# The skip count carried by the bit tile: one product per position sum instead of two, in a four-layer graph kernel

## The chip, the cores and the metric

The kernel runs on one core of a Trainium2 chip. The metric is the device time of one launch in microseconds; the median of several runs is compared. An execution under the hardware profiler gives the profile; its times are called "the profile" below. TensorE (PE) multiplies, VectorE (DVE) and ScalarE (ACT) work on tiles, SyncE (SP) issues the transfers.

## The reference

Sixteen graphs of N = 1024 nodes with D = 64 features pass through four layers, each of the form x = x + layer(relu(layernorm(x)), adj). Layers 1 to 3 are a weighted mean over neighbours, an attention with eight heads whose scores get the adjacency added, and a plain graph convolution. Layer 0 is the one that matters here. It thins the adjacency, and then takes for every node and every feature a weighted sum of the three quartiles over the node's remaining neighbours:

```python
vals = jnp.where(valid[..., None], x[:, None, :, :], big)
sv = jnp.sort(vals, axis=2)
m = valid.sum(-1)
for tau, wt in zip([0.25, 0.5, 0.75], [0.25, 0.5, 0.25]):
    pos = jnp.clip(tau * (m - 1.0), 0.0)
    lo, hi = floor(pos), ceil(pos)
    frac = pos - lo
    agg = agg + wt * (gather(sv, lo) * (1.0 - frac) + gather(sv, hi) * frac)
```

So for each node, feature and each of six positions (lo and hi of three quartiles) the kernel has to find the neighbour that has just that many smaller neighbours ahead of it.

## The kernel before, in words

Each feature of a graph is sorted once, so that every node has a rank. The 1024 ranks of a feature are cut into 64 buckets (NBK) of 16 places (BKW). For a block of 512 nodes, `group` (L704) counts by matmuls with the thinned adjacency (`valid`) how many neighbours lie in each bucket up to a given one (`cum`), and builds two halves (`c0`, `c1`) of a 16-bit word that tells which places of a bucket are occupied.

The inner work is done in 1536 steps (L776): 16 graphs x 8 groups of 8 features x 2 blocks of 512 nodes x 6 positions q. A step has three parts, and the loop of `picks` (L900) calls them for three different steps: `compare(n)`, `bits(n - 1)`, `value(n - 2)`.

- `compare` (L804) asks on VectorE which buckets lie below the wanted position (`le`), masks the two halves with it (`wa` L812, `wb` L814), and sums them over the buckets on TensorE. The PSUM tile `prep` then holds, for each node, feature and each of 16 places, the same word: its low bits are the occupied places of the right bucket, and its high bits are a count of places to skip. `val` holds the candidates' values. ScalarE copies `prep` to the float32 tile `wi`, adding 1 from a bias column (L840), and `val` to `vs` (L842).
- `bits` (L845) extracts on VectorE one bit of the word for each row: shift left by a number of the row's own (the column `to30`), and keep bit 30 alone. Read as a float, the result is 2 where the place is occupied and 0 elsewhere. TensorE then forms the position sum `pz` by two products: with `nth` (L853), which gives each row half of the sum of the bits of its block up to its own place, and a large negative number if its own place is occupied, and with `plus_k` (L854), a scaled identity applied to the high half of `wi`, which adds the skip count.
- `value` (L857) compares `pz` with one number, 97, and multiplies the value by the outcome (L861). After six positions TensorE gathers the six results (`agg`, L867).

The constants `to30`, `nth`, `plus_k` and `shifts` are made once at the start (L218 to L230 and L280 to L295). `prep`, `val` and `pz` take turns in two PSUM buffers (tag `pa`); `wi`, `bit` and some other tiles take turns in four buffers (tag `a2`).

Beside these steps run two other streams: the ranking and thinning for the next graph (`background`, L959), advanced once per step, and the layers 1 to 3 of the graph that is finished (`layers`, L1250). The last lines set the pace by hand: each step adds 0.42 to a sum that is due, and layers 1 to 3 issue pieces with prices of 0.2 to 1.0 as long as something is due (L1257 to L1261). The code gives every instruction its engine and a priority by its place; the order on each engine's queue is then settled when the program is built, with two hand-made bindings (`adjoining`, L399, keeps a run of matmuls together, and `issue_after` puts one behind another). Each engine runs its queue in that order.

Of the kernel before, what the change touches and what calls it, by code (L numbers as in the profile page):

```python
# [8 lines left out]
F32 = mybir.dt.float32  # L9
BF = mybir.dt.bfloat16  # L10
HP = mybir.dt.float16
F8 = mybir.dt.float8e4
I32 = mybir.dt.int32
I16 = mybir.dt.int16
U8 = mybir.dt.uint8
AF = mybir.ActivationFunctionType
OP = mybir.AluOpType
# [4 lines left out]
P = 128  # L22
# [6 lines left out]
KHI = 65536.0  # L29
# [4 lines left out]
FIRST = 127.0  # L34
# [4 lines left out]
def tile_preln_adj_stack(  # L39
# [30 lines left out]
    nc = tc.nc  # L70
# [8 lines left out]
    const = ctx.enter_context(tc.tile_pool(name="const", bufs=1))  # L79
# [20 lines left out]
    def pa(name, shape=(P, 512), dt=F32):  # L100
        return ps.tile(list(shape), dt, tag="pa", bufs=2, name=name)
# [22 lines left out]
    def sc(name, shape=(P, P), dt=F32):  # L124
        return scrp.tile(list(shape), dt, name=name)
# [3 lines left out]
    identf = const.tile([P, P], F32, name="identf")  # L129
# [9 lines left out]
    for b_ in range(N.bit_length() - 1):  # L139
        up = N.bit_length() - 2 - 2 * b_  # L140
        nc.vector.tensor_scalar(
            rev_b, rev_i, 1 << b_, abs(up), op0=OP.bitwise_and,
            op1=OP.logical_shift_left if up >= 0 else OP.logical_shift_right,
# [62 lines left out]
    same = scr_f[:, 1, :]  # L206
# [4 lines left out]
    fplr = bits_reversed(fpl, 4, P, "fpl")  # L211
    ppl = sc("ppl", (P, P), I32)
    nc.vector.tensor_scalar(ppl, prow_i, 15, None, op0=OP.bitwise_and)
    pplr = bits_reversed(ppl, 4, P, "ppl")
    nc.vector.tensor_scalar(pblk, prow_i, 4, None, op0=OP.logical_shift_right)
    nc.vector.tensor_tensor(same, pblk, fblk, OP.is_equal)

    to30 = const.tile([P, 1], I32, name="to30")  # L218
    nc.vector.tensor_scalar(to30, pplr[:, 0:1], 15.0, None, op0=OP.add)


    tri = scr_f[:, 2, :]
    nc.vector.tensor_tensor(tri, pplr, fplr, OP.is_le)
    nc.vector.tensor_tensor(tri, tri, same, OP.mult)
    nc.vector.tensor_scalar(tri, tri, 0.5, None, op0=OP.mult)
    nth = const.tile([P, P], BF, name="nth")
    nc.vector.scalar_tensor_tensor(nth, identf, -32.0, tri, op0=OP.mult, op1=OP.add)

    plus_k = const.tile([P, P], BF, name="plus_k")
    nc.vector.tensor_scalar(plus_k, identf, 1.0 / KHI, None, op0=OP.mult)  # L230


    sel_t = const.tile([P, 2, 32], F32, name="sel_t")
# [43 lines left out]
    nc.vector.tensor_scalar(bkt, prow_i[:, 0:1], 1, None, op0=OP.logical_shift_right)  # L277
    nc.vector.tensor_scalar(off[:, 0:1], bkt, 8.0, -SHIFT, op0=OP.mult, op1=OP.add)
    nc.vector.tensor_scalar(off[:, 1:2], bkt, 0.0, None, op0=OP.is_equal)
    shifts = const.tile([P, 7], F32, name="shifts")  # L280
    nc.vector.tensor_scalar(
        shifts[:, 0:1], off[:, 0:1], -1.0, None, op0=OP.mult
    )
# [7 lines left out]
    )  # L291
    nc.vector.tensor_scalar(shifts[:, 3:4], shifts[:, 2:3], FINE, None, op0=OP.mult)
    nc.vector.memset(shifts[:, 4:5], -0.5)
    nc.vector.memset(shifts[:, 5:6], 1.0)
    nc.vector.memset(shifts[:, 6:7], 2.0 * (160.0 - FIRST) + 2.0)  # L295

    def at_row(dst, terms):

# [97 lines left out]
    def act(out_, in_, func=AF.Copy, **kw):  # L396
        nc.scalar.activation(out_, in_, func, **kw)  # L397

    def adjoining(made):  # L399

        first = next(made)
        with tc.issue_after(first.ins), tc.high_priority():
            for _ in made:
                pass
# [213 lines left out]
    def positions(valid):  # L618

        m1 = sb.tile([P, N], I16, tag="m1", bufs=1, name="m1")
        for t in range(NH):
            pm = pa("pm")
            adjoining(
                nc.tensor.matmul(pm, ones, valid[t][:, j, :], start=j == 0, stop=j == C - 1)
                for j in range(C)
            )  # L630
            nc.vector.tensor_scalar(m1[:, t * 512 : (t + 1) * 512], pm, -1.0, None, op0=OP.add)
            if t < NH - 1:
                yield None
        n6 = a2("n6", (P, N), I16)
        nc.vector.tensor_scalar(n6, m1, q_tau, q_add, op0=OP.mult, op1=OP.add)
        nc.vector.tensor_scalar(n6, n6, 3, None, op0=OP.logical_shift_right)
        kq = sb.tile([P, N], HP, tag="kq", bufs=2, name="kq")
        nc.scalar.copy(kq, n6)
        yield kq
        krow = []  # L640
        for q in range(NQ):

            krow.append(sb.tile([P, N], I16, tag="krow", bufs=NQ, name="krow"))
            for t in range(NH):
                hs = slice(t * 512, (t + 1) * 512)
                pk = pb("pkr")
                nc.tensor.matmul(pk, sel_q[:, q, :], kq[:, hs], start=True, stop=True)
                act(krow[q][:, hs], pk, AF.Identity, scale=-2.0 / KHI, bias=shifts[:, 6:7])
            if q < NQ - 1:
                yield None  # L650
        yield krow
        nr = a2("nr", (P, N), I16)
        nc.vector.tensor_scalar(nr, m1, r_tau, None, op0=OP.mult)
        nc.vector.tensor_scalar(nr, nr, 3, None, op0=OP.bitwise_and)
        coef = sb.tile([P, N], BF, tag="coef", bufs=1, name="coef")
        nc.vector.tensor_scalar(coef, nr, w_frac, w_one, op0=OP.mult, op1=OP.add)
        yield coef
# [112 lines left out]
    def picks():  # L770
# [33 lines left out]
        def compare(n):  # L804
            b, g, t, q = steps[n]
            el = els[b]
            hs = slice(t * 512, (t + 1) * 512)
            cum, c1, c0 = tables[b, g, t]
            le = a4("le", (P, 4, 512), HP)
            nc.vector.tensor_tensor(le, cum, bc(el.krow[q][:, None, hs], [P, 4, 512]), OP.is_lt)  # L810
            wa = a4("wa", (P, 4, 512), HP)
            nc.vector.tensor_tensor(wa, le, c0, OP.mult)  # L812
            wb = a4("wb", (P, 4, 512), HP)
            last = nc.vector.tensor_tensor(wb, le, c1, OP.mult)  # L814
            while owing:
                owing.pop()(last)
            prep, val = pa("prep"), pa("val")

            rounds = [
                (prep, [sel_w[:, 1, :]] * 4, [wb[:, pp, :] for pp in range(4)]),  # L820
                (prep, [sel_w[:, 0, :]] * 4, [wa[:, pp, :] for pp in range(4)]),
            ] + [
                (val, [el.tab[:, i, 4 * g + pp, :] for pp in range(4)], [le[:, pp, :] for pp in range(4)])
                for i in range(2)
            ]
            nc.tensor.matmul(
                prep, sel_q[:, q, :], el.kq[:, hs], start=True, stop=False, skip_group_check=True
            )

            def made():  # L830
                for i, (dst, w, r) in enumerate(rounds):
                    for pp in range(4):
                        yield nc.tensor.matmul(  # L833
                            dst[32 * pp : 32 * pp + 32, :], w[pp], r[pp], start=i == 2, stop=i in (1, 3),
                            tile_position=(0, 32 * pp), skip_group_check=True,
                        )

            adjoining(made())
            wi = a2("wi")
            act(wi, prep, AF.Identity, bias=shifts[:, 5:6])  # L840
            vs = sb.tile([P, 512], F32, tag="v", bufs=7, name="vs")
            act(vs, val, AF.Copy, scale=1.0 / UP)  # L842
            state[n] = [wi, vs]

        def bits(n):  # L845
            wi, vs = state[n]
            bit = a2("bit", dt=I32)
            nc.vector.tensor_scalar(  # L848
                bit, wi.bitcast(I32), to30, 0x40000000, op0=OP.logical_shift_left, op1=OP.bitwise_and
            )  # L850
            pz = pa("pz")
            up = lambda x: x.bitcast(BF).rearrange("p (n two) -> p n two", two=2)[:, :, 1]
            nc.tensor.matmul(pz, nth, up(bit), start=True, stop=False)  # L853
            nc.tensor.matmul(pz, plus_k, up(wi), start=False, stop=True)  # L854
            state[n] = [pz, vs]

        def value(n):  # L857
            b, g, t, q = steps[n]
            el = els[b]
            pz, vs = state.pop(n)  # L860
            nc.vector.scalar_tensor_tensor(vs, pz, 97.0, vs, op0=OP.is_equal, op1=OP.mult)  # L861
            vs_of[q] = vs
            if q < NQ - 1:
                return
            agg = pb("agg")
            adjoining(
                nc.tensor.matmul(  # L867
                    agg[32 * (q_ % 4) : 32 * (q_ % 4) + 32, :], sel_t[:, q_ // 4, :], vs_of[q_],
                    start=q_ < 4, stop=q_ > 1, tile_position=(0, 32 * (q_ % 4)),
                    skip_group_check=True,  # L870
                )
                for q_ in range(NQ)
            )
            def weigh(behind):
                hs = slice(t * 512, (t + 1) * 512)
                w = a2("w")
                with tc.issue_after(behind.ins) if behind else ExitStack():
                    nc.vector.tensor_tensor(w, agg, el.coef[:, hs], OP.mult)
                acc = pb("acc", (8, 512))
                nc.tensor.matmul(acc, sel_c, w, start=True, stop=True)  # L880
                nc.scalar.copy(w[:8, :], acc)
                nc.sync.dma_start(el.z[t * D + 8 * g : t * D + 8 * g + 8, t, :], w[:8, :])

            owing.append(weigh)
# [15 lines left out]
        for n in range(last + 2):  # L900
            b, g, t, q = steps[min(n, last - 1)]
# [397 lines left out]
```

## Time and profile before

| what | us |
|---|---|
| median of three runs | 12745.85 |
| lowest, highest | 12739.58, 12749.53 |
| the profiled execution | 12739.76 |
| its span, first to last instruction | 12738.0 |
| setup and first graph's preparation | 0 to 360 |
| the 1536 steps, with layers 1 to 3 beside them | 360 to 12320 |
| layers of the last graph | 12320 to 12738 |

A group's row gives the line, the engine and operation, the tile written and the tiles read, shape and type of both, the count, the busy time in us, the mean duration of one in ns, and then the time for which the engine stood idle just before these instructions and what ended it. `L397` is the line of a helper through which all activations go, so they are told apart by their tiles. A matmul's duration is a modelled latency: a following matmul starts before it is over.

### The profile page before, as it was taken

How to read it: one execution, taken by the hardware profiler on the slowest of the kernel's cores; microseconds unless marked ns; L12 is line 12 of the kernel's file. 1: busy time of each engine (PE TensorE's matmuls, PEld its weight loads, DVE VectorE, ACT ScalarE, POOL GpSimd, SP SyncE). 2: the span in 40 equal slices, each digit the busy share in tenths (PEclk: the TensorE clock that was granted, in tenths of full speed). 3: DMA queues.
4: the chain of work that ended last, by engine and by line, in shares of the span. 5: the costliest groups of instructions: out<-in, count | busy, mean ns of one | idle time of the engine just before them, and what ended most of it. 6: DMA issues, size and time to landing. Idle time of an engine off the chain costs nothing.

```text
span 12738.0 us, 220547 instructions
## 1 busy us (share of the span) xinstructions
PE 11508.7 (90%) x86209; PEld 5414.4 (43%) x86209; DVE 11510.5 (90%) x19675; ACT 9625.0 (76%) x17026; POOL 1.4 (0%) x10
## 2 busy tenths in 40 slices
PE   0789999999899998999999999999999999999988
PEld 0224444444444444444444444444444444444445
DVE  8999989899898989989899998999989899887863
ACT  0557877777777787778877788787777778788866
POOL 0000000000000000000000000000000000000000
PEclk9999999999999999999999999999999999999999
DMA  3012121221212112121221212112121121202021
GB/s 105 29 41 71 52 89 56 72 72 55 83 54 94 54 55 85 51 92 57 68 72 59 88 55 81 60 62 83 55 84 56 62 84 57 94 30 70 28 71 60
DMA packets 503192, 841.31 MB, mean 66 GB/s; under 512 B 238720, under 2 KB 273664, under 8 KB 502144
## 3 DMA queue, kind: packets, MB, share of 16 engines
q1 hardware_dynamic: 502144, 827.20, 20.2%
q8 instruction: 675, 11.06, 0.4%
q14 instruction: 373, 3.06, 0.1%
HBM read 616.27 MB, written 206.57 MB: 65 GB/s over the span
## 4 chain that ended last, share of the span: by engine, by line
DVE 29%; PE 28%; ACT 10%; issue 5%; DMA 1%; SPq 0%; DVEq 0%; ACTq 0%
DVE wa L812 5%; PE px L726 4%; DVE wb L814 4%; DVE le L810 4%; DVE s L1191 4%; PE ao L1203 3%; PE pcols L450 2%; ACT s L397 2%; DVE vs L861 2%; PE sp L1182 2%; PE prep L833 2%; PE val L833 2%; DVE bit L848 2%; PE agg L867 1%; PE two L1069 1%
## 5 line engine op out<-in xcount | busy, mean ns | idle before, releaser
L812 DVE TENSOR_TENSOR wa<-le,c 128x2048 f16<-128x2048 f16 x1536 | 1878.1, 1223 | 250.2 <-PE prep L833 190.0
L726 PE MATMUL px<-valid,cw 128*128 128x512 fp8e4 x8192 | 1977.2, 381 | 0.0
L810 DVE TENSOR_TENSOR le<-cum,krow 128x2048 f16<-128x2048 int16 x1536 | 1875.1, 1221 | 11.0 <-PE val L833 8.9
L814 DVE TENSOR_TENSOR wb<-le,c 128x2048 f16<-128x2048 f16 x1536 | 1876.6, 1222 | 1.5 <-PE prep L833 1.5
L397 ACT ACTIVATE c<-px,shifts 128x512 f16<-128x512 f32 x2048 | 1414.2, 695 | 308.6 <-PE px L747 162.8
L397 ACT ACTIVATE wi<-prep,shifts 128x512 f32<-128x512 f32 x1536 | 1066.7, 694 | 357.7 <-PE prep L833 271.4
L397 ACT ACTIVATE s<-s,nm 128x1024 f32<-128x1024 f32 x1024 | 1168.2, 1143 | 211.5 <-DVE nm L1191 202.1
L726 PEld LDWEIGHTS <-cw 128*128 128x128 f16 x8192 | 799.8, 98 | 1094.2 <-issue 202.7
L1182 PE MATMUL sp<-kT,qT 64*128 64x512 f32 x4096 | 1164.7, 642 | 69.2 <-DVE nm L1191 67.7
L450 PE MATMUL pcols<-identf,s 128*128 128x128 f32 x8192 | 1130.6, 280 | 105.4 <-ACT eT L453 57.6
L397 ACT ACTIVATE high<-px,shifts 128x512 f16<-128x512 f32 x1024 | 713.0, 696 | 653.0 <-PE px L726 650.4
L861 DVE SCALAR_TENSOR_TENSOR vs<-pz,vs 128x512 f32<-128x512 f32 x1536 | 1057.8, 689 | 161.1 <-PE pz L854 140.1
L450 PEld LDWEIGHTS pcols<-identf,s 128*128 128x128 f32 x8192 | 888.2, 141 | 594.8 <-ACT eT L453 266.7
L833 PE MATMUL val<-le,tab 128*32 128x512 f16 x12288 | 1105.8, 385 | 26.8 <-DVE vs L861 17.1
L453 ACT COPY eT<-pcols 128x512 f32<-128x512 f32 x2048 | 1107.0, 599 | 15.5 <-PE pcols L450 13.6
L1203 PE MATMUL ao<-eT,v 128*64 128x128 f32 x16384 | 1054.8, 276 | 36.7 <-ACT eT L453 32.9
L397 ACT ACTIVATE vs<-val 128x512 f32<-128x512 f32 x1536 | 925.8, 603 | 156.6 <-PE val L833 82.9
L1203 PEld LDWEIGHTS ao<-eT,v 128*64 128x64 f32 x16384 | 899.3, 137 | 305.3 <-ACT eT L453 232.2
L1191 DVE CUSTOM_DVE_ANT_0 s<-sp,ad,nm 128x512 f32<-128x512 f32 x1024 | 728.4, 750 | 112.0 <-PE sp L1182 111.5
L1191 DVE CUSTOM_DVE_ANT_0 s<-sp,ad 128x512 f32<-128x512 f32 x1024 | 681.6, 689 | 141.7 <-PE sp L1182 105.4
L833 PE MATMUL prep<-wb,sel_w 128*32 128x512 f16 x6144 | 643.8, 392 | 125.9 <-DVE wb L814 122.3
L397 ACT ACTIVATE low<-px,shifts 128x512 f16<-128x512 f32 x1024 | 709.7, 697 | 54.4 <-PE px L738 52.8
(266 smaller groups left out, 18922.2 us busy)
## 6 DMA issues: line engine op xcount, KB each, us to landing
ad<-in_adj_dram SPq DMA_DIRECT2D x768, 512.0 KB
adjT_d<-aT SPq DMA_DIRECT2D x128, 512.0 KB
aT<-adjT_d SPq DMA_DIRECT2D x128, 512.0 KB
md<-sm SPq DMA_DIRECT2D x216, 256.0 KB
sb<-md SPq DMA_DIRECT2D x216, 256.0 KB
rem_d<-rem SPq DMA_DIRECT2D x128, 256.0 KB
left_d<-nb SPq DMA_DIRECT2D x128, 256.0 KB
lr<-left_d SPq DMA_DIRECT2D x256, 128.0 KB
```

What stands on the lines that cost most here:

```text
L397: nc.scalar.activation(out_, in_, func, **kw)
L450: nc.tensor.transpose(pt[:, c, :], ad[:, (4 * s + c) * P : (4 * s + c + 1) * P], identf)
L453: nc.scalar.copy(aT[:, 4 * s : 4 * s + 4, :], pt)
L726: yield nc.tensor.matmul(px[pp], w[:, j, :], valid[:, j, :], start=False, stop=j == C - 1, skip_group_check=True,)
L810: nc.vector.tensor_tensor(le, cum, bc(el.krow[q][:, None, hs], [P, 4, 512]), OP.is_lt)
L812: nc.vector.tensor_tensor(wa, le, c0, OP.mult)
L814: last = nc.vector.tensor_tensor(wb, le, c1, OP.mult)
L833: yield nc.tensor.matmul(dst[32 * pp : 32 * pp + 32, :], w[pp], r[pp], start=i == 2, stop=i in (1, 3), tile_position=(0, 32 * pp), skip_gr ...
L861: nc.vector.scalar_tensor_tensor(vs, pz, 97.0, vs, op0=OP.is_equal, op1=OP.mult)
L1182: nc.tensor.matmul(sps[e], qT[e * D : (e + 1) * D, i * P : (i + 1) * P], kT[e * D : (e + 1) * D, hs], start=True, stop=True,)
L1191: nc.vector.tensor_tensor_reduce(ss[e][:, hs], sps[e], ad[:, hs], -1.0, 3.0e38 if t == 0 else nms[e], op0=OP.add, op1=OP.min, accum_out=nm,)
L1203: nc.tensor.matmul(ao[e * D : (e + 1) * D, :], v[:, j, e * D : (e + 1) * D], eTs[e][:, j, :], start=j == 0, stop=j == C - 1, tile_position ...
```

## The change

The place of each block of 16 rows whose bit-reversed number is 15 needs no bit in the sum. Its row of the bit tile is used for the skip count. The shift becomes 0 for these rows, and the mask, until now one constant for all rows, becomes a second column of `to30`: bit 30 for the other rows, the upper 16 bits for these. `nth` gets the scaled skip count's weight in these rows, for all columns of the block, and other numbers on its diagonal and in the columns of the free rows. The product with `plus_k` goes. The number compared with is 80. `wi` is made by a plain copy, without the bias column; `shifts` loses that column.

```diff
-    to30 = const.tile([P, 1], I32, name="to30")
-    nc.vector.tensor_scalar(to30, pplr[:, 0:1], 15.0, None, op0=OP.add)
+    to30 = const.tile([P, 2], I32, name="to30")
+    field = sc("field", (P, P))
+    nc.vector.tensor_scalar(field, pplr, 15.0, None, op0=OP.is_equal)
+    keep = sc("keep", (P, P))
+    nc.vector.tensor_scalar(keep, field, -1.0, 1.0, op0=OP.mult, op1=OP.add)
+    nc.vector.tensor_scalar(to30[:, 0:1], pplr[:, 0:1], 15.0, keep[:, 0:1], op0=OP.add, op1=OP.mult)
+    nc.vector.tensor_scalar(
+        to30[:, 1:2], field[:, 0:1], -65536.0 - 1073741824.0, 1073741824.0, op0=OP.mult, op1=OP.add
+    )
...
+    nc.vector.scalar_tensor_tensor(tri, identf, -40.5, tri, op0=OP.mult, op1=OP.add)
+    nc.vector.tensor_tensor(tri, tri, keep, OP.mult)
+    nc.vector.tensor_tensor(field, field, same, OP.mult)
+    nc.vector.scalar_tensor_tensor(tri, field, 1.0 / KHI, tri, op0=OP.mult, op1=OP.add)
+    nc.vector.tensor_scalar(field, fplr, 15.0, -0.5, op0=OP.is_equal, op1=OP.mult)
+    nc.vector.tensor_scalar(field, field, 1.0, None, op0=OP.add)
     nth = const.tile([P, P], BF, name="nth")
-    nc.vector.scalar_tensor_tensor(nth, identf, -32.0, tri, op0=OP.mult, op1=OP.add)
-
-    plus_k = const.tile([P, P], BF, name="plus_k")
-    nc.vector.tensor_scalar(plus_k, identf, 1.0 / KHI, None, op0=OP.mult)
+    nc.vector.tensor_tensor(nth, tri, field, OP.mult)
...
-    nc.vector.memset(shifts[:, 5:6], 1.0)
...
-            act(wi, prep, AF.Identity, bias=shifts[:, 5:6])
+            nc.scalar.copy(wi, prep)
...
-                bit, wi.bitcast(I32), to30, 0x40000000, op0=OP.logical_shift_left, op1=OP.bitwise_and
+                bit, wi.bitcast(I32), to30[:, 0:1], to30[:, 1:2], op0=OP.logical_shift_left, op1=OP.bitwise_and
...
-            nc.tensor.matmul(pz, nth, up(bit), start=True, stop=False)
-            nc.tensor.matmul(pz, plus_k, up(wi), start=False, stop=True)
+            nc.tensor.matmul(pz, nth, up(bit), start=True, stop=True)
...
-            nc.vector.scalar_tensor_tensor(vs, pz, 97.0, vs, op0=OP.is_equal, op1=OP.mult)
+            nc.vector.scalar_tensor_tensor(vs, pz, 80.0, vs, op0=OP.is_equal, op1=OP.mult)
```

More of the change, by code (lines that the diff above doesn't have):

```diff
@@ L279, in tile_preln_adj_stack @@
     nc.vector.tensor_scalar(off[:, 1:2], bkt, 0.0, None, op0=OP.is_equal)
-    shifts = const.tile([P, 7], F32, name="shifts")
+    shifts = const.tile([P, 6], F32, name="shifts")
     nc.vector.tensor_scalar(
@@ L293, in tile_preln_adj_stack @@
     nc.vector.memset(shifts[:, 4:5], -0.5)
-    nc.vector.memset(shifts[:, 5:6], 1.0)
-    nc.vector.memset(shifts[:, 6:7], 2.0 * (160.0 - FIRST) + 2.0)
+    nc.vector.memset(shifts[:, 5:6], 2.0 * (160.0 - FIRST) + 2.0)
     def at_row(dst, terms):
@@ L647, in positions @@
                 nc.tensor.matmul(pk, sel_q[:, q, :], kq[:, hs], start=True, stop=True)
-                act(krow[q][:, hs], pk, AF.Identity, scale=-2.0 / KHI, bias=shifts[:, 6:7])
+                act(krow[q][:, hs], pk, AF.Identity, scale=-2.0 / KHI, bias=shifts[:, 5:6])
             if q < NQ - 1:
```

## The prediction

> **What bounds the kernel now.** I read the page first (busy times, then the chain that ended last), then the busy times by stage, then the groups by shape, the waits, and last the order of time around the instructions that the change touches. From the page:
>
> ```profile
> PE 11508.7 (90%) x86209; PEld 5414.4 (43%) x86209; DVE 11510.5 (90%) x19675; ACT 9625.0 (76%) x17026; POOL 1.4 (0%) x10
> ...
> DVE 29%; PE 28%; ACT 10%; issue 5%; DMA 1%; SPq 0%; DVEq 0%; ACTq 0%
> ```
>
> TensorE and VectorE are busy for the same time, and on the chain they share the blame: 29 and 28. The page's shares add up to 73, because the chain is followed back only so far; of what it covers, VectorE has 29/73 = 40%, TensorE 28/73 = 38%, ScalarE 10/73 = 14%. By stage (columns: PE, PEld, DVE, ACT, POOL):
>
> ```profile
> 360.00:12320.00 11960.00, 11099.41 (x83196) 5146.06 (x83189) 11077.68 (x18490) 9303.32 (x16418) 0.00 (x0) 0.99 0.20 65
> ```
>
> All 1536 position sums lie in these 11,960 us, 7.79 us each. VectorE idles for 11,960.0 - 11,077.7 = 882 us there, 7%. Who holds it up is in the waits (total, times, longest):
>
> ```profile
> DVE wa L812 <- PE prep L833: 190.0, 152, 5.8
> DVE vs L861 <- PE pz L854: 140.1, 109, 5.2
> DVE s L1191 <- PE sp L1182: 114.0, 85, 3.8
> DVE w L878 <- PE agg L867: 87.7, 45, 7.7
> ...
> PE prep L833 <- DVE wb L814: 122.3, 157, 3.8
> PE pz L853 <- DVE bit L848: 88.2, 132, 2.8
> ```
>
> These are the waits in that stage. The four largest waits of VectorE, 532 us, all end with TensorE, and one of them ends with the very product that the change takes out (L854). TensorE in turn waits for VectorE, less. So two engines take turns at being late, and neither alone is the bound.
>
> **What the Trainium skill says.** "ScalarE: Activation LUTs", section "What ACT_TABLE_LOAD costs": an activation with constants takes 186 ns plus 0.833 ns per element, and each per-partition operand adds about 93 ns. The trace agrees: 694 ns with the bias column against 599 for the copy of the same shape. "TensorE: Matmul & The Clock Gate", "Back-to-back issue gap", gives 216 ns between two 512-column products as the gap of single ones; the trace has 0.22 to 0.24 us. "VectorE: DVE Perf Modes", "The perf-mode tier table", puts a float32 tensor_scalar between SBUF tiles at two elements per cycle; the 484 ns of the bit extraction against 689 for two-input float32 operations of the same size fit that. The pages that I read give no price for a second per-partition scalar on VectorE; I take that from the trace.
>
> **The change, part by part.** The rows that price it, groups by shape:
>
> ```profile
> L848 DVE TENSOR_SCALAR bit<-wi,to 128x512 int32<-128x512 int32 x1536 | 743.0, 484 | 0.8 <-ACT cw L397 0.7
> ...
> L453 ACT COPY eT<-pcols 128x512 f32<-128x512 f32 x2048 | 1107.0, 599 | 15.5 <-PE pcols L450 13.6
> L397 ACT ACTIVATE wi<-prep,shifts 128x512 f32<-128x512 f32 x1536 | 1066.7, 694 | 357.7 <-PE prep L833 271.4 <-PE val L833 49.0 <-issue 23.8
> ```
>
> *The second product (L854) goes.* A matmul's listed 390 ns is its latency; what it costs in a queue is the distance between starts:
>
> ```profile
> 6013.36 0.40 PE L853 MATMUL pz<-bit,nth 128*128 128x512 bf16 x1
> 6013.60 0.39 PE L854 MATMUL pz<-wi,plus_k 128*128 128x512 bf16 x1
> 6013.82 0.38 PE L747 MATMUL px<-high,dif 128*128 128x512 f16 x1
> ```
>
> From 6013.60 to 6013.82 is 0.22 us. 1536 x 0.22 = 338 us of TensorE time. Its weight load lies beside the product ahead of it and is counted at nothing; should some of the loads be exposed, the gain is up to 98 ns larger for each (at most 150 us over all). On the path, at TensorE's share of 38%: 338 x 0.38 = 128 us.
>
> *The bias column leaves the copy of the position word (wi).* 694 - 599 = 95 ns, x 1536 = 146 us of ScalarE, x 14% on the path = 20 us.
>
> *The mask becomes a column (L848).* The operation now reads two per-partition scalars where it read one and a constant. The trace has all three kinds in a row, two, one and none, none of them held up:
>
> ```profile
> 11584.31 0.55 DVE L635 TENSOR_SCALAR n<-m,q_tau,q_add 128x1024 int16<-128x1024 int16 x1
> 11584.77 0.48 DVE L848 TENSOR_SCALAR bit<-wi,to 128x512 int32<-128x512 int32 x1
> 11585.16 0.42 DVE L636 TENSOR_SCALAR n<-n 128x1024 int16<-128x1024 int16 x1
> 11585.50 0.69 DVE L1191 CUSTOM_DVE_ANT_0 s<-sp,ad 128x512 f32<-128x512 f32 x1
> ```
>
> Starts are 0.46, 0.39 and 0.34 us apart, durations 0.55, 0.48 and 0.42: each scalar column costs about 0.06 us. (L635 is 1024 two-byte elements, four per cycle if the 0.42 of L636 is that rate; L848 is 512 four-byte ones at two per cycle, the same number of cycles.) 1536 x 0.06 = 92 us of VectorE, x 40% = 37 us on the path. No trace row has two columns of int32 in a bitwise operation. The low bound is no cost at all, if the second column is fetched with the first (they are neighbours in one tile); the high bound is that the operation drops to one element per cycle, 0.69 + 0.06 = 0.75 us. I take 0.06, since L635 keeps its rate with two columns.
>
> *Setup.* Nine operations on 128x128 tiles come and two go, one on a column comes and a memset goes; in the trace such rows follow each other at 0.14 to 0.20 us. About 2 us, once, in the first 20 us of the run, where VectorE works without pause: all of it on the path.
>
> *Waits.* None is added and no DMA or queue is moved. L861 now waits for one product instead of two; its place as last wait is taken by the first product. The position word's buffer is given back after the bit extraction instead of after the product; the only visible waits for such a buffer (e behind pz, L853) are 6 us, so I count nothing, and with nothing hidden there is nothing to lose. The products' PSUM pair is shared with prep and val; the waits of prep and val behind L861 are 19 us, also too small to count.
>
> *Sum.* 128 + 20 - 37 - 2 = 109 us. That is a first-order number: a path that is shortened is soon overtaken by another one, so gains come out smaller than share times saving, and costs don't. I choose 85% of the gains: 0.85 x 148 = 126, less 39, gives 87 us. The profiled execution took 12,739.76 us, of which the span is 12,738.0; the median of the runs is 6 us above it. 12,739.8 - 87 = 12,653, in terms of the median 12,659; I say **12,655**.
>
> **The rivals.**
>
> *TensorE counts for more than its share (15%).* The chain names one engine where two are nearly equally late. If VectorE's long waits for TensorE (532 us of 882) are taken as the sign of who leads, TensorE has some 65% and VectorE 25% of the path: 338 x 0.65 + 20 - 23 - 2 = 215 us, 12,525. For it: L861 behind L854 is the second largest wait. Against it: TensorE waits for L848 and L814 too.
>
> *VectorE is the bound and TensorE's time is hidden (9%).* One mechanism: between wa, bit and wb VectorE's queue is full, bit grows by 0.06 us, wb and everything queued behind it starts later, and TensorE merely waits longer for wb. Price: up to 92 + 2 us, 12,834. With shares p for TensorE and 0.79 - p for VectorE it decides where 338p + 20 = 92 x (0.79 - p) + 2, at p = 0.13. For it: VectorE is 93% busy in the loop and three of the four largest groups are its own. Against: the chain gives TensorE 0.38, three times that.
>
> *The order changes (9%).* The instructions' order on each engine is set when the program is built: in the trace the bit extraction lies between wa and wb, though the code issues it after both. One product and some durations fewer may deal a different order, with no sign to expect; it could eat what is gained: 12,740.
>
> *The mask column takes the operation out of its faster mode (3%).* 0.75 - 0.48 = 0.27 us, x 1536 = 415 us more on VectorE. It would then lead: at a share of 60%, 249 - 126 = 123 us slower, 12,863.
>
> That the change doesn't do what it says I give no chance: the call of the second product is gone from the code; its count in the trace will tell.
>
> **How the numbers follow.** The forecast has 64%, with 12,590 to 12,715 as its own range: at the fast end all of the first-order sum and a second scalar that is nearly free, at the slow end half of the gains and the scalar in full. About 0.2%, 25 us, is what a measurement of this kernel can tell from no change. Of the forecast's 64, 60 lie below 12,720; with the second case 15 and 1 from a lucky order, faster has 76%. Within 0.2%: 4 of the forecast, 7 of the changed order, 1 of the VectorE case: 12%. Slower: 8 of the VectorE case, 3 of the slow mask, 1 of the order: 12%. For 8 in 10 I go from 12,510 (most of the second case) to 12,745 (most of the changed orders), and leave out the two slow cases.
>
> **What would show it right or wrong.** No row of L854; one product per sum, 1536 in all. The row of wi is a COPY near 600 ns. The row of bit is near 545 ns; 480 would mean a free second scalar, 750 the slow mode. VectorE's busy time in the loop grows by about 90 us, while its idle time falls from 882 to some 700; the wait of L861 for pz falls most. If instead VectorE's idle time stays and waits of TensorE for bit and wb grow by 300 us, VectorE was the bound. If groups that the change doesn't touch move their waits by more than the sum does, it was the order.

## The result, and the profile after

| | before | after |
|---|---|---|
| median, us | 12745.7 (5 runs) | 12683.74 (5 runs) |
| lowest, highest | 12738.82, 12749.53 | 12677.98, 12693.13 |
| profiled execution, its span | 12739.76, 12738.0 | 12693.13, 12691.3 |

The ratio is 0.9954 with a 95% interval from 0.9943 to 0.9966: 62 us faster at the medians, 43 to 73 us by the interval. The profiled execution after is the slowest of its five; it lies 9 us above the median, which matters where its sums are compared with a difference of 62.

The same lines of the page as before the change:

```profile
PE 11305.5 (89%) x84673; PEld 5334.0 (42%) x84673; DVE 11575.8 (91%) x19682; ACT 9481.6 (75%) x17026; POOL 1.4 (0%) x10
...
DVE 34%; PE 25%; ACT 9%; issue 4%; DMA 1%; ACTq 0%; SPq 0%; DVEq 0%
```

There are 1536 matmuls fewer, and the balance on the chain has tipped: VectorE's share went from 29 to 34, TensorE's from 28 to 25. The stage of the 1536 sums, which now ends near 12,270 us (columns as before: PE, PEld, DVE, ACT, POOL):

```profile
360.00:12270.00 11910.00, 10892.33 (x81680) 5063.87 (x81679) 11142.11 (x18491) 9160.71 (x16419) 0.00 (x0) 0.98 0.20 65
```

VectorE is busy for 64 us more in it and idle for 11,910.0 - 11,142.1 = 768 us, 114 less than before. The waits in that stage (total, times, longest):

```profile
DVE wa L821 <- PE prep L842: 155.3, 125, 7.0
DVE vs L869 <- PE pz L862: 99.4, 100, 3.3
DVE s L1199 <- PE sp L1190: 92.3, 69, 6.2
DVE w L886 <- PE agg L875: 85.7, 47, 10.5
...
PE prep L842 <- DVE wb L823: 174.3, 196, 6.8
PE pz L862 <- DVE bit L857: 89.3, 137, 3.5
```

The four waits of VectorE for TensorE fell from 532 to 433 us, most of all the one of the comparison for the position sum, 140 to 99. In return TensorE waits longer for wb, 122 to 174. The two operations that changed, groups by shape:

```profile
L849 ACT COPY wi<-prep 128x512 f32<-128x512 f32 x1536 | 910.3, 593 | 438.8 <-PE prep L842 354.6
...
L857 DVE TENSOR_SCALAR bit<-wi,to 128x512 int32<-128x512 int32 x1536 | 827.2, 539 | 0.3 <-ACT cw L406 0.3
```

In order of time, a single product now lies between TensorE's other work, and the next one starts 0.24 us after it:

```profile
6008.49 0.40 PE L862 MATMUL pz<-bit,nth 128*128 128x512 bf16 x1
6008.73 0.38 PE L756 MATMUL px<-high,dif 128*128 128x512 f16 x1
```

One figure moved that the prediction did not consider, the granted TensorE clock over the span (its mean, as a share of full speed). Before, and after:

```profile
core 0: 12738.0 us, clock 0.987
...
core 0: 12691.3 us, clock 0.978
```

It falls in every build that has one product (below).

### The profile page after: what moved, and what is told of

The parts are those of the page before. It is cut to its first block, busy times and chain, and to the rows that moved or that the text cites. A ratio compares the mean times of both kernels' runs of the same rounds, so it can differ in the third digit from the quotient of the medians.

```text
span 12691.3 us, 217061 instructions
## 1 busy us (share of the span) xinstructions
PE 11305.5 (89%) x84673; PEld 5334.0 (42%) x84673; DVE 11575.8 (91%) x19682; ACT 9481.6 (75%) x17026; POOL 1.4 (0%) x10
## 4 chain that ended last, share of the span: by engine, by line
DVE 34%; PE 25%; ACT 9%; issue 4%; DMA 1%; ACTq 0%; SPq 0%; DVEq 0%
DVE wa L821 5%; DVE wb L823 5%; DVE le L819 5%; DVE s L1199 5%; PE px L735 4%; DVE vs L869 3%; PE ao L1211 2%; PE pcols L459 2%; DVE bit L857 2%; ACT s L406 2%; PE sp L1190 2%; PE prep L842 2%; PE two L1077 1%; PE agg L875 1%; PE val L842 1%
## 5 line engine op out<-in xcount | busy, mean ns | idle before, releaser
L823 DVE TENSOR_TENSOR wb<-le,c 128x2048 f16<-128x2048 f16 x1536 | 1867.5, 1216 | 3.0 <-PE prep L842 3.0
L849 ACT COPY wi<-prep 128x512 f32<-128x512 f32 x1536 | 910.3, 593 | 438.8 <-PE prep L842 354.6
L857 DVE TENSOR_SCALAR bit<-wi,to 128x512 int32<-128x512 int32 x1536 | 827.2, 539 | 0.3 <-ACT cw L406 0.3
```

## The experiments

The change has three parts: the mask column (VectorE), the plain copy (ScalarE) and the product that goes (TensorE). I made each alone on the kernel before, and took each alone out of the kernel after. With the two kernels themselves these are all eight combinations of the parts; one of them was built in two ways. The kernel before had medians of 12,743 to 12,746 us beside them.

**The mask column alone.**

```diff
-    to30 = const.tile([P, 1], I32, name="to30")
-    nc.vector.tensor_scalar(to30, pplr[:, 0:1], 15.0, None, op0=OP.add)
+    to30 = const.tile([P, 2], I32, name="to30")
+    nc.vector.tensor_scalar(to30[:, 0:1], pplr[:, 0:1], 15.0, None, op0=OP.add)
+    nc.vector.tensor_scalar(to30[:, 1:2], pplr[:, 0:1], 0.0, 1073741824.0, op0=OP.mult, op1=OP.add)
...
-                bit, wi.bitcast(I32), to30, 0x40000000, op0=OP.logical_shift_left, op1=OP.bitwise_and
+                bit, wi.bitcast(I32), to30[:, 0:1], to30[:, 1:2], op0=OP.logical_shift_left, op1=OP.bitwise_and
```

> The kernel before with one part of the change alone: the mask of the bit extraction is a second column of to30, with the old constant in every row, so the output is the same. Theory of the prediction (each engine pays by its share of the path): bit lasts 545 ns in place of 484, 92 us more on VectorE, 37 us slower. VectorE is the bound: 92 us slower. TensorE leads: 23 us slower. The mean granted TensorE clock stays near 0.987.

Measured: 12,822.44 us, ratio 1.006 [1.0048, 1.0073], 76 us slower. The groups by shape:

```profile
L848 DVE TENSOR_SCALAR bit<-wi,to 128x512 int32<-128x512 int32 x1536 | 843.1, 549 | 2.7 <-ACT cw L397 1.7 <-ACT wi L397 0.9
```

The operation keeps its rate, as forecast; but twice the forecast share of its cost arrives, 76 of 92 us in place of 37. That is between the first two theories.

**The plain copy alone.**

```diff
-            act(wi, prep, AF.Identity, bias=shifts[:, 5:6])
+            nc.scalar.copy(wi, prep)
```

> The kernel before with one part alone: wi is made by a plain copy. The one that the bias column added to the position word is left out, so the outputs are others. Theory of the prediction: wi lasts 600 ns in place of 694, 146 us less on ScalarE, 14% of it on the path: 17 to 20 us faster. VectorE is the bound: no change. If ScalarE counts for more than its share of the chain, over 50 us faster.

Measured: 12,751.62 us, ratio 1.0005 [0.9997, 1.0014]. ScalarE is busy for 128 us less (9,625.0 to 9,497.0 on the page) and the time doesn't move. The theory of shares, with its 17 to 20 us, is not confirmed here. That VectorE is the bound would fit, but fails on the next build.

**The product alone.**

```diff
-            nc.tensor.matmul(pz, nth, up(bit), start=True, stop=False)
-            nc.tensor.matmul(pz, plus_k, up(wi), start=False, stop=True)
+            nc.tensor.matmul(pz, nth, up(bit), start=True, stop=True)
```

> The kernel before with one part alone: the second product (L854) is taken out, and with it the skip count from the position sums, so the outputs are others. Theory of the prediction: 338 us less on TensorE, 38% on the path, of which 85% is kept: 109 us faster. VectorE is the bound: no change, and waits of TensorE for bit and wb grow by 300 us. TensorE leads: about 220 us faster. A fourth theory, formed on the profile after (its mean clock is 0.978, not 0.987): with less to do TensorE is granted its full clock less often; then the clock falls to about 0.978 here too, and part of the 109 us is given back.

Measured: 12,648.72 us, ratio 0.9927 [0.9913, 0.994], 97 us faster. The waits of this kernel:

```profile
PE prep L833 <- DVE wb L814: 142.1, 178, 3.9
DVE vs L861 <- PE pz L853: 124.6, 109, 3.9
...
PE pz L853 <- DVE bit L848: 75.6, 124, 2.7
```

TensorE's waits for bit and wb grew by 7 us together (122.3 + 88.2 to 142.1 + 75.6), not by 300: VectorE is not the bound. The gain is not 220 either. The first theory's 109 is nearest. The clock of this profile:

```profile
core 0: 12631.4 us, clock 0.982
```

In the other four executions it was 0.980 or 0.981. So the fourth theory is right that the clock falls, by more than half of what it expected; whether that gave back a part of the gain, this build alone doesn't tell.

**A nudge in the setup.**

```diff
+    nc.vector.tensor_scalar(plus_k, plus_k, 1.0, None, op0=OP.mult)
```

> The kernel before with one more operation of 0.2 us on VectorE in the setup (plus_k times one); nothing in the loop is changed. It tells how far a new order of the queues, settled when the program is built, moves the time by itself. If the order matters little: within 10 us of before. If the order is a cause of the size of the parts: 30 us or more, either way.

Measured: 12,748.61 us, ratio 1.0002 [0.9994, 1.001]. It doesn't test what it was made for: in the trace all 17,026 instructions of ScalarE stand in the same place as before, and so do those of VectorE once the setup is over: the order came out the same. What it shows is that one and the same order, built anew, repeats within 3 us. In the mask, copy and product builds, by contrast, only some 6,000 to 8,900 of ScalarE's 17,026 stand where they stood.

**The kernel after with the old constant mask.**

```diff
-                bit, wi.bitcast(I32), to30[:, 0:1], to30[:, 1:2], op0=OP.logical_shift_left, op1=OP.bitwise_and
+                bit, wi.bitcast(I32), to30[:, 0:1], 0x40000000, op0=OP.logical_shift_left, op1=OP.bitwise_and
```

> The kernel after with the old constant as mask for all rows. The free rows then pass no skip count, so it is left out of the position sums and the outputs are others. What stays of the change is one product fewer and the plain copy. If the three parts simply add, as measured each alone on the kernel before (mask 76 us, product -97, copy +5): 12,608 us, 92 us faster than before. If VectorE's second scalar is cheap inside the change, for example because the order of the queues there hides it: 12,650 to 12,684. Bit lasts 482 ns; the clock stays near 0.98.

Measured: 12,635.5 us, ratio 0.9915 [0.9902, 0.9929]. The mask costs 12,683.7 - 12,635.5 = 48 us inside the change, 28 less than alone. The time lies 27 us above the 12,608 that adding the parts gives; they do not simply add.

**The kernel after with a second product.**

```diff
+    none_k = const.tile([P, P], BF, name="none_k")
+    nc.vector.memset(none_k, 0.0)
...
-            nc.tensor.matmul(pz, nth, up(bit), start=True, stop=True)
+            nc.tensor.matmul(pz, nth, up(bit), start=True, stop=False)
+            nc.tensor.matmul(pz, none_k, up(wi), start=False, stop=True)
```

> The kernel after with a second product per position sum put back where it was (weights of zero on the high half of wi, added to pz); the output is the same. If the parts add: 12,684 + 97 = 12,781. If the saving on TensorE was worth less inside the change than alone, 12,720 to 12,750. Theory of the clock: the half-clock time, 566 us in the kernel after against 334 before, goes back to about 350 with the product, whatever the time is; if it stays near 560, it isn't TensorE's load that sets it.

Measured: 12,787.35 us, ratio 1.0037 [1.0024, 1.0049]. The product is worth 12,787.4 - 12,683.7 = 104 us inside the change. And the clock comes back with it, as the theory of the clock expected:

```profile
core 0: 12780.8 us, clock 0.986
```

**The second product ahead of the first.** In the kernel after, and in the kernel before with its own two products:

```diff
+            nc.tensor.matmul(pz, none_k, up(wi), start=True, stop=False)
+            nc.tensor.matmul(pz, nth, up(bit), start=False, stop=True)
```

> The kernel after with the same zero product put ahead of the real one, where it needs wi alone and not the bit tile, so that it can run while TensorE waits for bit. TensorE's queue holds as much as in a_two_products. If what the second product costs is TensorE's time: within 15 us of a_two_products. If it is the delay between bit and the value behind it: near the kernel after, 12,684 to 12,710.

> The kernel before with its two products in the other order: plus_k on wi first, which is ready earlier, then nth on bit. All work stays, and the output is the same. If the second product costs TensorE's time alone: 12,746, within 15 us. If it costs the delay between bit and value: up to 50 us faster, with the wait of L861 for pz smaller than 140 us.

Measured: 12,813.11 us for the first, ratio 1.0055 [1.0042, 1.0068], and 12,730.04 us for the second, ratio 0.999 [0.9983, 0.9996]. A product that needn't wait for bit costs no less: 129 us above the kernel after, where it costs 104 in its old place. That is 26 more, outside the 15 that were expected. In the kernel before the exchange gains only 13 us, although the wait of L861 for pz fell by 26 (between 360 and 12,200 us from 139 to 113). So what the second product costs is TensorE's time and not mainly the delay behind bit. Why the one is 26 us worse and the other 13 us better isn't shown; both have an order of their own. With all work kept, then, a new order together with a new place of one product moved the time by 13 and by 26 us.

**The missing combinations, and the nudge again.** Back to the bias in the kernel after; mask and copy on the kernel before; the nudge on two builds:

```diff
-            nc.scalar.copy(wi, prep)
+            act(wi, prep, AF.Identity, bias=none)
```

> The kernel after with the bias column put back into the copy of prep (a column of zeros, so the output is the same): mask column and one product, without the plain copy. If the plain copy is worth nothing, as alone on the kernel before (+5): 12,684. If it is worth what the two-product kernel with mask and copy suggests (12,787 against 12,822 with the mask alone): 12,719. The share theory of the prediction: 17 to 20 us above after, 12,702.

> The kernel before with mask column and plain copy, both products as they were (the added one is left out of the position word, so the outputs are others). It has the same work in the loop as a_two_products, whose setup and numbers differ. If order and setup matter little: 12,787 within 15 us. If the parts add as measured alone: 12,746 + 76 + 5 = 12,827.

> The kernel with the mask column alone (12,822) and one more operation of 0.2 us in the setup. If the 76 us are the price of the second scalar: 12,822 within 10 us. If part of them is the order of the queues that this one build came out with: lower, 12,780 to 12,800, as the prediction's share theory has it (12,783).

> The kernel after and one more operation of 0.2 us in the setup (nth times one). If the order of the queues matters little: 12,684 within 10 us. If the result of this one build is in part the luck of its order: 25 us or more, either way.

Measured: 12,687.42, 12,783.74, 12,819.91 and 12,676.31 us; ratios 0.9955 [0.9943, 0.9968], 1.0031 [1.002, 1.0043], 1.006 [1.0048, 1.0073] and 0.9947 [0.9933, 0.996]. The plain copy is worth 4 us inside the change. Mask and copy on the kernel before give what the kernel after with two products gives, 12,784 and 12,787: the same loop work, and the traces show ScalarE's queue in the same order in all 17,026 places; different setup and numbers make no more than 4 us. The nudges again leave ScalarE's order untouched and the times within 3 and 7 us, so the 76 us of the mask alone belong to that build and its order, and are no accident of one run.

All eight combinations, medians in us:

| | two products | one product | the product's worth |
|---|---|---|---|
| neither | 12,746 | 12,649 | 97 |
| plain copy | 12,752 | 12,636 | 116 |
| mask column | 12,822 | 12,687 | 135 |
| both | 12,784 | 12,684 | 100 |

Each part's worth is the difference between two builds that differ in it alone. Averaged over its four settings, the product gains 112 us, the mask costs (76 + 32 + 38 + 48)/4 = 49 and the copy gains (-6 + 13 + 38 + 4)/4 = 12. Three plain sums from these averages leave residues of up to 16 us.

## Why the prediction was right, and where its sizes were off

The prediction was right in direction and in mechanism. The product's removal makes the kernel faster in all four settings, by about a third of the TensorE time that it frees, and the mask column makes it slower in all four, so VectorE pays a part back. 12,684 lies in the range and 29 us above the point. By the prediction's steps:

- *The second product.* Priced at 338 us of TensorE time, of which 128 were put on the path and 109 kept. Measured 97 to 135, on average 112, and 104 as the last part taken out. The share that arrives is 112/338 = 33% on average and 29 to 40% in single settings; 38% with the discount of 15% was 32%. Right in size. But the clock fell with the product, which the prediction had not considered. So the share itself isn't confirmed: a larger share, less what a lower clock takes back, would look the same.
- *The mask column.* Priced at 0.06 us each, 92 us. The trace confirms the price: with the mask column alone VectorE is busy for 11,594.6 us against 11,510.5, 84 us more, at the same rate. Put on the path at 40%, 37 us; measured 48 inside the change, 49 on average, but 32 to 76 in single settings. The term was too small, and why is open. That the change itself moves the balance toward VectorE (its share of the chain after is 34/73 = 47%) does not explain it: with two products, where the share was 40%, the mask costs 76 and 32 us, 54 on average; with one product 38 and 48, 43 on average. Nor is a share of the chain a steady figure. The kernel after with a nudge has the same work and the same order, yet its chain is followed back over 14% of the span only, and names TensorE first:

```profile
PE 7%; ACT 3%; DVE 3%; issue 1%; DMA 0%; ACTq 0%; SPq 0%; DVEq 0%
```

- *The plain copy.* 20 us on paper, 17 after the discount; 4 inside the change, 12 on average, and between -6 and 38. The kernel after with the bias put back has this row:

```profile
L406 ACT ACTIVATE wi<-prep,none 128x512 f32<-128x512 f32 x1536 | 1069.6, 696 | 388.3 <-PE prep L842 311.9
```

  Against it the plain copy of the kernel after takes 159 us less (910.3), and ScalarE waits 50 us longer in front of it (438.8), most of it for the same product of TensorE. A third of what ScalarE saves there it waits.
- *The sum.* 109 us before and 87 after the discount; measured 62. Taken out of the kernel after one at a time, product, mask and copy give 104 - 48 + 4 = 60. Against the prediction's 109 - 39 + 17 that is 5 from the product, 9 from the mask with its setup, and 13 from the copy. No step failed; the mask's share and the copy's were mis-sized. That it came out so near is in part luck: made one at a time on the kernel before, the same parts give 97 - 76 - 6 = 15.
- *VectorE's idle time* was to fall from 882 to some 700 us; it fell to 768. Its busy time in the loop was to grow by about 90 us and grew by 64; the last paragraph of this document has the two parts of that. The wait that was to fall most did.
- *The rivals.* VectorE as the bound: refuted by the product alone. TensorE for more than its share: refuted at the size that was given to it, 97 in place of 220. The slow mask: refuted by 539 ns.
- *The clock* was put at nothing, by silence. How much time its fall costs no build separates, but the executions of one kernel give a hint. Of 60 of the kernel before, the 28 with a mean clock of 0.987 have a median of 12,741 us and the 8 with 0.985 one of 12,750: 9 us for 0.002. If the same held between builds, the fall by 0.009 would go with some 40 us (an estimate), hidden in what the product was measured at. That the low clock lengthens an execution, and that the two don't merely have a common cause, isn't shown.
- *The order of the queues* remains. My test of it was the nudge, and that left the order alone. By the averages above the eight builds deviate by up to 16 us from a plain sum; whether that is their order or a true interplay of the three engines is open, since each part also deals its own order. The two exchanges of products, 13 and 26 us at equal work, show that an order and a place alone can be worth that much.

## What to carry to other kernels

Where two engines alternate as the last to finish, work taken off one of them arrives in part only, and work laid on another is paid in part. The engine's share of the chain was a fair first guess for the product here (38% forecast before any discount, 29 to 40% measured), and a poor one for a small part: of the mask's 92 us between 35 and 83% arrived, against 40%. So price both sides by the distance between starts, not by durations, and make each part alone as well as take it out of the whole: the mask cost 76 us in one setting and 32 to 48 in the others. A test of the order of the queues must first be seen to change it.

## What the runs showed of the hardware

- A second per-partition scalar on an int32 tensor_scalar of 128x512 costs 0.06 us and leaves the rate as it is. The mean duration is 480 to 489 ns in the six builds with one column and 537 to 549 ns in the eight with two. In the kernel after the next start comes 0.46 us later, where it came after 0.39 before:

```profile
6021.45 0.54 DVE L857 TENSOR_SCALAR bit<-wi,to 128x512 int32<-128x512 int32 x1
6021.91 0.68 DVE L705 TENSOR_TENSOR e<-k,rk 128x1024 f16<-128x1024 f16 x1
```

- The mean granted TensorE clock was lower in every build without the second product: 0.978 to 0.982 in the profiles of five builds with one product, 0.983 to 0.987 in the nine with two, and 0.986 again when a product of zeros was put back. The Trainium skill says as much of this clock ("TensorE: Matmul & The Clock Gate", Part 1, the HAM clock gate: it is set by how busy TensorE has been recently), and these runs agree in sign. From 0.987 to 0.978 is 0.009 x 12,691 = 114 us of full-speed time, a third of the 338 us that the product freed. TensorE's busy time fell by 11,508.7 - 11,305.5 = 203 us in the kernel after, and by 239 with the product alone, not by 338; how much of the difference is the clock isn't separated.
- The durations of one profile shift together, and this is no change of speed. At equal work and order wa lasts 1,227 ns with the mask alone and 1,216 with the nudge added, but the distance from its start to the next, where nothing holds that up, has a median of 1,135 or 1,136 ns in all fourteen builds. VectorE's busy time hardly moves with it: 11,594.6 and 11,591.9 us in these two. So the 64 us by which it grew in the loop are no noise. Over the whole span the product alone takes it from 11,510.5 to 11,489.8, 21 less, and the mask, between the kernel after with the constant mask and the kernel after, from 11,490.4 to 11,575.8, 85 more.
